# Zeros through the matrix engine, one group's statistics later, and batch norm rows widened by another engine

## The chip, the cores and the metric

The kernel runs on one core of a Trainium2 chip. A core has a matrix engine (TensorE, PE in the profile), a vector engine (VectorE, DVE), a scalar engine (ScalarE, ACT), a general engine (GpSimd, POOL) and a queue engine (SyncE, SP) that here only issues DMAs; ACT and POOL issue DMAs too. PE reads its operands from the on-chip memory SBUF and writes its products to [...]another one, PSUM, from which DVE and ACT take them away. The metric is device time in microseconds of one execution of the whole program.

## The reference

The input is `x`, 128 samples of 128 nodes with 256 channels, in float32, and an adjacency matrix for each sample. Two layers follow one another, each of the form `x = x + f(relu(layernorm(x)))`. Cut to its first part, which is all that the change touches, the first layer is

```python
h  = relu(layernorm(x))                     # per node, over 256 channels
c  = relu(bn1(conv1d(h, conv1_w, width 1))) # a 256x256 product per node
c  = bn2(conv1d(c, conv2_w, width 17))      # a convolution along the nodes
xc = relu(c + h)                            # then messages, a GRU, the second layer
```

`bn1` multiplies each output channel by a scale and adds a shift. Everything after (messages along an adjacency computed from the data, a GRU, and a second layer of five small graph convolutions) is unchanged.

## The kernel before, in words

The samples go in groups of four, numbered q = 0 to 31; sixteen groups make a batch (`bat`). The width-17 convolution is done in the frequency domain: stage A brings a batch into it, stage B multiplies there, and a third stage goes back and does everything else.

**Stage A, for one group** (`stage_a`, L390 to L443). SP loads the group's input into a tile `xa` (four DMAs of 128 KB, L382; four such tiles exist, so group q+4 takes the place of group q). `moments` (L265 to L275) computes mean and variance on DVE, four pairs of instructions, and the inverse root on POOL (L274); `normalize` (L277) applies them on DVE. PE transposes the group (`ph`, L411), ACT applies the ReLU into `hTa` (L413, two tiles, each of which POOL also stores to DRAM, L416), PE multiplies by the width-1 weights `c1w` (`pc`, L422), DVE adds the shift row `brow` (L425), ACT applies the ReLU (L427), PE multiplies by the Fourier matrix (`pf`, L433), and DVE and ACT copy the result into `X` (L439, L441).

**Before the first group** `fold` (L282 to L307) works bn1 into `c1w`. The scale and the shift stand as columns (one number per partition) and are needed as rows. So DVE widens each of four columns to 128x128 (`wide`, L301), PE multiplies it with the identity (`prow`, L302), DVE multiplies `c1w` by the scale rows (L306) and copies the shift rows to `brow` (L307). `fold` also computes the moments of group 0 and normalises it (L303).

**Beside stage A** `tap_weights` (L461) brings the 17 taps of the second convolution into the frequency domain: 32 steps of four products (`pw`, L477), in four rounds of eight. The taps of round n are loaded into one of two tiles `wt` by SP and POOL (`load_taps`, L452), so those of round 2 can be loaded only when the last products of round 0 are done. POOL stores the results (`wfd`, L489).

**The order** of all this is planned on the host. Each program (`stage_a(q)` of up to three groups, `tap_weights`) is a Python generator that issues instructions and then yields two numbers, the PE time that it has just used and the time after which it wants to be asked again. A planner (`Order`, L176) keeps a clock of its own from these numbers and asks whichever program is due. [...]The line that concerns us is in `stage_a`: a group that has no moments yet computes them when it is asked (L397 to L402), and the load of group q+1 is issued when group q starts (L392).

Of the kernel before, what the change touches and what calls it, by code (L numbers as in the profile page):

```python
# [9 lines left out]
FP = mybir.dt.float32  # L10
AF = mybir.ActivationFunctionType
# [4 lines left out]
B, N, D = 128, 128, 256  # L16
# [3 lines left out]
P = 128  # L20
# [187 lines left out]
def kernel(ctx: ExitStack, tc: tile.TileContext, x, adj, consts, vecs, w_se, conv1_w,  # L208
                    conv2_w, w_msg, b_msg, w_ih, w_hh, W1, W2, b2, fusion_w, out):
    nc = tc.nc  # L210
# [7 lines left out]
    ptmp = ctx.enter_context(tc.tile_pool(name="ptmp", bufs=5, space=PSUM))  # L218
# [15 lines left out]
    def c(name):  # L234
        a, b = CAT[name]
        return cst[:, a:b]

    def v(name, i=None):
        a, b = VAT[name]
        return vec[:, a:b] if i is None else vec[:, a + i:a + i + 1]  # L240
# [24 lines left out]
    def moments(src, tag):  # L265

        st = f2.tile([P, 4, 6], FP, tag=tag + "st", name="st", bufs=4)
        mv = f2.tile([P, 4, 2], FP, tag=tag + "mv", name="mv", bufs=4)
        rs = f2.tile([P, 4], FP, tag=tag + "rs", name="rs", bufs=4)
        for t in range(4):  # L270
            nc.vector.bn_stats(st[:, t], src[:, t])
            nc.vector.bn_aggr(mv[:, t], st[:, t])
        nc.vector.tensor_scalar(rs, mv[:, :, 1], EPS, None, op0=ALU.add)
        nc.gpsimd.tensor_tensor(rs, rs, c("mhalf")[:, :4], ALU.pow)  # L274
        return mv, rs  # L275

    def normalize(dst, src, mv, rs):  # L277
        for t in range(4):
            nc.vector.tensor_scalar(dst[:, t], src[:, t], mv[:, t, 0:1], rs[:, t:t + 1],
                                    op0=ALU.subtract, op1=ALU.mult)  # L280

    def fold():  # L282


        s = cp.tile([P, 4], FP, name="s_bn")
        t = cp.tile([P, 4], FP, name="t_bn")
        for i, bn in enumerate(("bn1", "bn2")):
            scl[bn], sft[bn] = s[:, 2 * i:2 * i + 2], t[:, 2 * i:2 * i + 2]
            nc.vector.tensor_scalar(scl[bn], v(bn + "_v"), EPS, None, op0=ALU.add)
        nc.gpsimd.tensor_tensor(s, s, c("mhalf")[:, :4], ALU.pow)  # L290
        MOM[0] = moments(XA[0], "a")
        load_taps(0, nc.gpsimd, nc.sync)
        for bn in ("bn1", "bn2"):
            nc.vector.tensor_mul(scl[bn], scl[bn], v(bn + "_g"))
            nc.vector.tensor_mul(sft[bn], v(bn + "_m"), scl[bn])
            nc.vector.tensor_sub(sft[bn], v(bn + "_b"), sft[bn])
        prow = ptmp.tile([P, 4, P], FP, tag="tmp", name="prow")
        wide = tw.tile([P, 4, P], FP, tag="wide", name="wide", bufs=1)
        for i, a in enumerate((scl["bn1"][:, 0:1], scl["bn1"][:, 1:2], sft["bn1"][:, 0:1],
                               sft["bn1"][:, 1:2])):  # L300
            nc.vector.tensor_copy(wide[:, i], a.to_broadcast([P, P]))  # L301
            nc.tensor.matmul(prow[:, i], wide[:, i], ident, start=True, stop=True)  # L302
        normalize(XA[0], XA[0], *MOM[0])  # L303
        nc.vector.tensor_add(brz, v("b_ih")[:, 0:4], v("b_hh")[:, 0:4])
        for k in range(2):
            nc.vector.tensor_mul(c1w[:, k], c1w[:, k], prow[:, 0:2].rearrange("p a c -> p (a c)"))  # L306
        nc.vector.tensor_copy(brow, prow[:, 2:4].rearrange("p a c -> p (a c)"))  # L307

    def fold_gates():

# [58 lines left out]
    brow = xf.tile([P, D], FP, name="brow")  # L369
# [15 lines left out]
    def load_xa(q):  # L385
        if q not in XA:
            XA[q] = LATE["ab"].tile([P, 4, D], FP, tag="xa", name=f"xa{q}", bufs=4)
            load_x(XA[q], q)

    def stage_a(q):  # L390
        ab = LATE["ab"]
        for n in range(q, min(q + 2, (q // BQ + 1) * BQ)):  # L392
            if n not in XA:
                load_xa(n)
                if n == q:
                    yield 0.0, 14.0 if q > BQ else 6.0
        if q not in MOM:  # L397
            if BQ < q < BQ + 3:
                yield 0.0, 11.0 * (q - BQ) - 10.0
            MOM[q] = moments(XA[q], "a")  # L400
            yield 0.0, 3.0
            normalize(XA[q], XA[q], *MOM[q])  # L402
            yield 0.0, 2.0
        while q - 2 >= q // BQ * BQ and q - 2 not in A_DONE:
            yield 0.0, 0.5
        xn = XA[q]
        hT = ab.tile([P, 2, 512], FP, tag="hTa", name=f"hTa{q}")
        for cc in range(2):
            ph = ptmp.tile([P, 4, GB, WIDE], FP, tag="tmp", name=f"ph{q}_{cc}")
            for t in range(4):  # L410
                nc.tensor.transpose(ph[:, t].rearrange("p j n -> p (j n)"),  # L411
                                    xn[:, t, cc * P:(cc + 1) * P], ident)
            nc.scalar.activation(  # L413
                hT[:, cc].rearrange("p (j t n) -> p t j n", j=GB, t=4), ph, AF.Relu)
        yield 0.9, 2.4
        nc.gpsimd.dma_start(out=hTd[q], in_=hT)  # L416
        h1 = ab.tile([P, GB, D], FP, tag="h1", name=f"h1{q}")
        for h in range(2):
            pc = ptmp.tile([P, 2, D], FP, tag="tmp", name=f"pc{q}_{h}")
            for i in range(2):  # L420
                for k in range(2):
                    nc.tensor.matmul(pc[:, i], hT[:, k, (2 * h + i) * N:(2 * h + i + 1) * N],  # L422
                                     c1w[:, k], start=(k == 0), stop=(k == 1))
            s = slice(2 * h, 2 * h + 2)
            nc.vector.tensor_tensor(h1[:, s], pc, brow[:, None, :].to_broadcast([P, 2, D]),  # L425
                                    ALU.add)
            nc.scalar.activation(h1[:, s], h1[:, s], AF.Relu)  # L427
            yield 1.75, 2.8 * h
        for h in range(2):
            for k in range(2):  # L430
                pf = ptmp.tile([P, 2, D], FP, tag="tmp", name=f"pf{q}_{k}_{h}")
                for i in range(2):
                    nc.tensor.matmul(pf[:, i, :F * NB], h1[:, 2 * h + i, k * P:(k + 1) * P],  # L433
                                     fwd, start=True, stop=True)
                g0 = (q % BQ * GB + 2 * h) * NB
                dst = X[:, k, :, g0:g0 + 2 * NB].rearrange("p f (g b) -> p f g b", b=NB)
                src = pf[:, :, :F * NB].rearrange("p g (f b) -> p f g b", b=NB)
                if (k, h) == (0, 0):
                    nc.vector.tensor_copy(dst, src)  # L439
                else:  # L440
                    nc.scalar.activation(dst, src, AF.Copy)  # L441
            yield 1.1, 0.0
        A_DONE.add(q)  # L443
# [3 lines left out]
    tws = [mid.enter_context(tc.tile_pool(name=f"tws{i}", bufs=1)) for i in range(3)]  # L447
    tw = mid.enter_context(tc.tile_pool(name="tw", bufs=2))
    wse = tw.tile([P, 2, 67], FP, tag="wse", name="wse", bufs=1)
    wts = []  # L450

    def load_taps(n, *engines):  # L452

        wt = tw.tile([P, 16, D], FP, tag="wt", name=f"wt{n}")
        src = conv2_w.rearrange("(r n i) t o -> n t r i o", r=4, n=4)[n]
        for r in range(4):
            engines[r % len(engines)].dma_start(out=wt[32 * r:32 * r + 16], in_=src[:16, r])
        engines[0].dma_start(out=wt[16::32], in_=src[16])
        wts.append(wt)
# [727 lines left out]
    load_xa(1)  # L1187
    load_xa(2)
    fold()
    beside = Lane([tap_weights()] + [early(q) for q in range(NQ)])  # L1190
    gates = Lane([fold_gates(), fold_fusion()], weight=0.5)
    for bat, (during_a, during_b) in enumerate(((0.66, 0.5), (0.2, 0.65))):
        if bat:
            take_turn("ab", 2, reuse_waits="tile")
        begin = Lane([stage_a(q) for q in range(bat * BQ, (bat + 1) * BQ)], ahead=3)
        beside.weight = during_a
        order.run(begin, beside, *[gates] * bat, until=begin)
        take_turn("xw", 3, reuse_waits="tile")
        products = Lane([stage_b(bat)])
        beside.weight = during_b  # L1200
        order.run(products, beside, *[gates] * bat, until=products)
# [52 lines left out]
```

## Time and profile before

| | |
|---|---|
| time, median of 3 runs | 2012.26 us (2009.02 to 2017.96) |
| time of the profiled execution | 2009.44 us |
| its span, first to last instruction | 2007.7 us |
| PE busy | 1960.1 us, 98% of the span |
| DVE, ACT, POOL busy | 67%, 34%, 33% |
| first product of the kernel's own (`prow`) | 9.93 us from the span's start |
| first product of stage B (`pa`) | 190.35 us |

Times inside the profile are counted in microseconds from the start of the span. A row of the order of time gives the start, the time until the last of the merged instructions ends, engine, line, operation, output and input; a bracket gives how long the engine had been idle and what released it. SPq and POOL rows named DMA_DIRECT2D are the issuing of a DMA, not its transfer. One float32 product appears as two PE records.

### The profile page before, as it was taken

To read this page: it belongs to the slowest core of one execution; us is meant where nothing else is said; L and a number is where in the kernel's file an instruction comes from. 1 tells how busy PE (TensorE), PEld (TensorE's weight loads), DVE (VectorE), ACT (ScalarE), POOL (GpSimd) and SP (SyncE) were. 2 spreads that over 40 slices of the span, in tenths; PEclk is the share of its full clock that TensorE was granted. 3 is DMA by queue.
4 is the path that set the end of the run, shared out by engine and by line. 5 is a ranking of instruction groups with operands and counts; after the bars stand their busy time and mean duration, and the time that the engine had idled before them with its cause. 6 is when DMAs were issued, how large, how long until landed. Compare 5 with 4: busy or idle time off the path is not lost.

```text
span 2007.7 us, 33356 instructions
## 1 busy us (share of the span) xinstructions
PE 1960.1 (98%) x12598; PEld 1625.4 (81%) x12598; DVE 1352.3 (67%) x3002; ACT 683.4 (34%) x1547; POOL 655.7 (33%) x897
## 2 busy tenths in 40 slices
PE   7999999999999999999999999999999999999998
PEld 5667888889888888878778878888888888888865
DVE  6775445885433576885885787778668867886652
ACT  4664222454222344222323232232323332322233
POOL 3452666332656111241331232222221322222320
PEclk9999999999999999999999999999999999999999
DMA  9997879744887743542433342443442433433331
GB/s 212 296 273 250 274 250 289 220 148 158 269 258 254 198 124 107 163 103 82 119 90 108 106 113 77 118 112 88 118 121 80 126 102 98 107 102 108 65 94 53
DMA packets 184106, 302.88 MB, mean 151 GB/s; under 512 B 28501, under 2 KB 131994, under 8 KB 183690
## 3 DMA queue, kind: packets, MB, share of 16 engines
q1 hardware_dynamic: 138762, 168.81, 28.9%
q0 software_dynamic: 44800, 131.66, 22.6%
q8 instruction: 100, 1.64, 0.3%
q14 instruction: 60, 0.49, 0.1%
q10 hardware_dynamic: 384, 0.28, 0.1%
HBM read 204.12 MB, written 109.05 MB: 156 GB/s over the span
## 4 chain that ended last, share of the span: by engine, by line
PE 87%; DVE 7%; DMA 3%; issue 1%; ACT 1%; SPq 1%; POOL 0%; DVEq 0%; ACTq 0%; POOLq 0%
PE p L755 41%; PE pa L531 7%; PE ph L1110 5%; PE pz L1119 5%; PE pm L642 5%; PE pc L422 4%; PE pb L531 3%; PE px L668 3%; PE pf L433 3%; PE pi L712 3%; PE pw L477 1%; PE py L1093 1%; PE ph L411 1%; DMA xa<-in_x 1%; PE pse L626 1%
## 5 line engine op out<-in xcount | busy, mean ns | idle before, releaser
L938 POOL DMA_DIRECT2D x1d<-xt x128 | 101.1, 815 | 467.2 <-DVE xt L936 454.9
L837 POOL DMA_DIRECT2D xt<-in_x x128 | 100.2, 789 | 173.8 <-DMA x1d<-xt 166.8
L563 DVE SCALAR_TENSOR_TENSOR y<-pa,kk 128x512 f32<-128x512 f32 x78 | 53.8, 690 | 151.2 <-ACT kk L562 151.1
L531 PE MATMUL pa<-wf,X 128*128 128x256 f32 x640 | 152.2, 381 | 0.0
L755 PE MATMUL p<-th,wrz 128*128 128x256 f32 x512 | 134.5, 385 | 0.0
L755 PE MATMUL p<-tc,wrz 128*128 128x256 f32 x512 | 131.4, 379 | 0.0
L755 PE MATMUL p<-tm,wrz 128*128 128x256 f32 x512 | 131.4, 379 | 0.0
L531 PEld LDWEIGHTS pa<-wf,X 128*128 128x128 f32 x640 | 118.1, 190 | 16.2 <-issue 2.0
L422 PE MATMUL pc<-c1w,hTa 128*128 128x256 f32 x512 | 121.2, 383 | 2.7 <-DVE X L439 1.5
L642 PE MATMUL pm<-wmsg,hT 128*128 128x256 f32 x512 | 121.5, 382 | 0.0
L1110 PE MATMUL ph<-yz,w 128*128 128x96 f32 (+3 forms) x640 | 109.3, 325 | 1.4 <-DVE yz L1095 1.4
L422 PEld LDWEIGHTS pc<-c1w,hTa 128*128 128x128 f32 x512 | 94.0, 191 | 19.9 <-DVE h L425 4.8
L755 PEld LDWEIGHTS p<-th,wrz 128*128 128x128 f32 x512 | 94.7, 190 | 19.1 <-issue 7.3
L1112 ACT ACTIVATE hh<-ph,vec 128x96 f32<-128x96 f32 (+3 forms) x160 | 63.6, 401 | 133.5 <-PE ph L1110 125.1
L724 ACT ACTIVATE xc<-xc,t_bn 128x256 f32<-128x256 f32 x128 | 58.2, 500 | 148.5 <-DVE xc L721 148.5
L755 PEld LDWEIGHTS p<-tc,wrz 128*128 128x128 f32 x512 | 97.3, 190 | 13.9 <-issue 0.8
L642 PEld LDWEIGHTS pm<-wmsg,hT 128*128 128x128 f32 x512 | 95.8, 190 | 15.2 <-ACT kk L562 1.4
L1119 PE MATMUL pz<-hh,w 128*128 128x96 f32 (+3 forms) x640 | 107.5, 322 | 0.7 <-DVE yz L1121 0.7
L755 PEld LDWEIGHTS p<-tm,wrz 128*128 128x128 f32 x512 | 97.3, 190 | 13.2
L1110 PEld LDWEIGHTS ph<-yz,w 128*128 128x128 f32 x640 | 88.3, 193 | 22.4 <-issue 15.6
L1119 PEld LDWEIGHTS pz<-hh,w 128*128 128x128 f32 x640 | 86.3, 191 | 18.6 <-DVE yz L1121 1.3
L755 PE MATMUL p<-hTc,wrz 128*128 128x256 f32 x384 | 99.3, 381 | 1.2 <-DVE z L829 1.2
(204 smaller groups left out, 4464.8 us busy)
## 6 DMA issues: line engine op xcount, KB each, us to landing
wf<-wfd SPq DMA_DIRECT2D x160, 256.0 KB
wfd<-ws POOLq DMA_DIRECT2D x64, 320.0 KB, 10.2
yd<-y POOLq DMA_DIRECT2D x80, 256.0 KB, 4.0
yt<-yd SPq DMA_DIRECT2D x64, 320.0 KB
w<-in_W SPq DMA_DIRECT2D x40, 512.0 KB
xa<-in_x SPq DMA_DIRECT2D x128, 128.0 KB
hTd<-hTa POOLq DMA_DIRECT2D x32, 512.0 KB, 6.6
hT<-hTd SPq DMA_DIRECT2D x32, 512.0 KB
```

Of the source, the lines that this page charges most:

```text
L422: nc.tensor.matmul(pc[:, i], hT[:, k, (2 * h + i) * N:(2 * h + i + 1) * N], c1w[:, k], start=(k == 0), stop=(k == 1))
L433: nc.tensor.matmul(pf[:, i, :F * NB], h1[:, 2 * h + i, k * P:(k + 1) * P], fwd, start=True, stop=True)
L531: nc.tensor.matmul(ps, xk(k), WF[f][:, k, s], start=(k == 0), stop=(k == 1))
L642: nc.tensor.matmul(pm[:, i], hT[:, k, j * N:(j + 1) * N], LATE["wmsg"][:, k], start=(k == 0), stop=(k == 1))
L668: nc.tensor.matmul(px[:, dc, i], msgs[h][:, i, dc * P:(dc + 1) * P], aT[:, 2 * h + i], start=True, stop=True)
L712: nc.tensor.matmul(pi[w * WIDE:(w + 1) * WIDE, :, :, n].rearrange("p k g c -> p g k c"), inv[:F, o:o + WIDE], yt[:, n // 2::2].rearrange(" ...
L755: nc.tensor.matmul(ps[:, m], w[:, i, k, m * P:(m + 1) * P], factor(i, x, t), start=first and j == 0, stop=last and j == len(n) - 1, skip_g ...
L837: nc.gpsimd.dma_start(out=xt[a * WIDE:(a + 1) * WIDE].rearrange("p b d c -> p (b d) c"), in_=slices(x[q * GB:(q + 1) * GB])[a])
L938: nc.gpsimd.dma_start(out=slices(x1d[q])[a], in_=xt[a * WIDE:(a + 1) * WIDE].rearrange("p b d c -> p (b d) c"))
L1110: nc.tensor.matmul(ph, w1[:, k, m * P:(m + 1) * P], yz[:, k, :, o:o + n], start=(k == 0), stop=(k == 1))
L1112: nc.scalar.activation(hh[:, m], ph, AF.Relu, bias=v("b1", g * 4 + m))
L1119: nc.tensor.matmul(pz, w2[:, g, m, cc * P:(cc + 1) * P], hs[g][:, m], start=(m == 0), stop=(m == 3))
```

## The change

Three edits, all in what runs before and during stage A of the first batch.

```diff
 def fold():
-            nc.vector.tensor_copy(wide[:, i], a.to_broadcast([P, P]))
+            nc.scalar.activation(wide[:, i], a.to_broadcast([P, P]), AF.Copy)
             nc.tensor.matmul(prow[:, i], wide[:, i], ident, start=True, stop=True)
...
-        nc.vector.tensor_copy(brow, prow[:, 2:4].rearrange("p a c -> p (a c)"))
+        nc.scalar.activation(brow, prow[:, 2:4].rearrange("p a c -> p (a c)"), AF.Copy)
...
 def stage_a(q):
         if q not in MOM:
+            if q == 2:
+                yield 0.0, 7.0
             if BQ < q < BQ + 3:
                 yield 0.0, 11.0 * (q - BQ) - 10.0
             MOM[q] = moments(XA[q], "a")
...
     wse = tw.tile([P, 2, 67], FP, tag="wse", name="wse", bufs=1)
     wts = []
+    idle = tws[2].tile([P, 4, 4, D], FP, tag="ws", name="idle")[:, 0, :3]
+    nc.gpsimd.memset(idle, 0.0)
+    pidle = ptmp.tile([P, 2, D], FP, tag="tmp", name="pidle")
+    for _ in range(5):
+        nc.tensor.matmul(pidle, idle[:, 2, :P], idle[:, :2], start=True, stop=True)
```

The four widenings and the copy to `brow` go from DVE to ACT. The group of index 2 waits seven units of the planner's clock before its moments are issued. And five products of zeros, 128x512 each, are issued to PE ahead of everything else; their result is read by nobody.

Because the planner decides with a running clock, the second edit also changes the order of what follows. In the program that is built, PE's order differs from the kernel before in its first 140 or so of 2868 rows (through the first rows of the third round of taps, all within stage A of the first batch) and is the same after that. In SP's queue, the load of group 7 now stands behind the loads of the taps of round 2, where it stood ahead of them; group 9 stands ahead of the late constants (L253 to L255) and group 11 ahead of the taps of round 3, where they stood behind them. In DVE's queue, the moments of group 7 stand directly after those of group 6 and ahead of the two additions of `brow` (L425) of group 5; the moments of group 10 stand directly after those of group 9.

## The prediction

> **What bounds the kernel now.** The page first: PE is busy in 98% of the span, and its chain of what ended last is 87% PE.
>
> ```profile
> span 2007.7 us, 33356 instructions
> PE   7999999999999999999999999999999999999998
> DMA  9997879744887743542433342443442433433331
> ```
>
> One slice is 50 us. So a microsecond of PE idleness saved or added early moves the end by as much; only the first slice has room; and there the DMA engines are as full as PE. Second, the order of time of the first 25 us.
>
> ```profile
> 9.66 0.36 DVE L301 COPY wide<-s_bn 128x128 f32<-128x128 f32 x2
> ...
> 9.93 2.08 PE L302 MATMUL prow<-cst,wide 128*128 128x128 f32 x8 [9.93 <-DVE wide L301]
> ...
> 12.05 0.75 DVE L306 TENSOR_TENSOR c1w<-c1w,prow 128x256 f32<-128x256 f32 x2 [0.32 <-PE prow L302]
> 12.72 0.42 DVE L307 COPY brow<-prow 128x256 f32<-128x256 f32 x1
> 13.05 0.42 DVE L271 BATCH_NORM_STATS2 st<-xa 128x6 f32<-128x256 f32 x1
> ...
> 15.48 0.43 DVE L271 BATCH_NORM_STATS2 st<-xa 128x6 f32<-128x256 f32 x1
> ...
> 17.82 0.68 DVE L425 TENSOR_TENSOR h<-pc,brow 128x512 f32<-128x512 f32 x1
> 18.42 2.66 DVE L279 TENSOR_SCALAR xa<-xa,mv,rs 128x256 f32<-128x256 f32 x8
> ...
> 21.00 0.68 DVE L425 TENSOR_TENSOR h<-pc,brow 128x512 f32<-128x512 f32 x1
> ...
> 27.59 1.04 PE L411 MATMUL ph<-cst,xa 128*128 128x128 f32 x8
> ```
>
> From 12 to 21.7 DVE sets the pace: two groups' moments (2.43 us each, 13.05 to 15.48 to 17.91) and eight normalisations stand before the additions that PE's group 1 needs; its `pc` starts at 22.89. From there PE is dense. Third, the queue engine, its order of time and its waits between 40 and 60 us.
>
> ```profile
> 28.65 13.45 SPq L382 DMA_DIRECT2D xa<-in_x  x8
> 57.69 1.26 SPq L457 DMA_DIRECT2D wt<-in_conv_w  x2
> 58.99 0.74 SPq L458 DMA_DIRECT2D wt<-in_conv_w  x1
> 59.83 2.13 SPq L382 DMA_DIRECT2D xa<-in_x  x4
> ...
> SPq L457 <- PE pw L477: 15.4, 1, 15.4
> ```
>
> SP stands 15.4 us before the taps of round 2, until PE's last product of round 0 (57.5). In this kernel groups 6 and 7 were loaded ahead of that wait; group 8 is the one behind it. Fourth, DVE after the taps of round 3, where the same happens to group 11:
>
> ```profile
> 112.36 0.43 DVE L271 BATCH_NORM_STATS2 st<-xa 128x6 f32<-128x256 f32 x1 [1.91 <-DMA xa<-in_x]
> ```
>
> PE lost 1.7 us to that at 113.5 and 0.8 at 117.
>
> **What the Trainium skill says.** "TensorE: Matmul & The Clock Gate", Part 1: PE's clock is halved until a window of about 3.4 us has been busy, and again after an idle one. The trace agrees: eight records of 128 columns took 2.08 us at 9.93 and 1.04 at 27.59; the granted-clock records begin full speed at 14.7 and show half speed for 3.4 us at 171.7, after 3.60 us of waiting. The same page (architectural detail) calls DVE and ACT strict FIFO. "Trainium Kernel Development and Optimization", Key Constraints: DMAs of SP, ACT and POOL share 16 engines and interleave. The trace: while POOL's stores ran (78 to 84 us) SP's queue moved 82 to 96 KB/us, alone (60 to 66) 130. "ScalarE: Activation LUTs", What ACT_TABLE_LOAD costs: 186 ns + 0.833 per element, 293 ns for 128; the trace's nearest row (aT, 128x128) has 281.
>
> **The change part by part.** Against the profiled execution (2009.44 for a span of 2007.7).
>
> *Zeros.* A memset of 768 columns on POOL, by the row of 848 columns (858 ns) 0.8 us, is done by about 1.5; POOL's next work is at 5.16. Five products of 512 columns: eight `pc` records of 256 take 1.82 us start to start, so a product of 512 takes 0.91, cold 1.8; together 4.6 to 9.1, over at 7 to 10.6, and `prow` is due at 9.3. If they wake the clock, `prow` and the first `ph` run at full speed; but `prow` is then awaited by nobody (DVE normalises group 0 until 11.4) and `ph` waits for that normalisation. Worth 0.3 us, between +0.7 (zeros late, clock cold) and -0.8. The PSUM bank and the `ws` tile that they use are next wanted long after.
>
> *ACT for DVE.* DVE loses four copies (0.54) and `brow` (0.42). ACT is idle there until 12.90; four at 0.28 start when the scale is ready (8.9) and end near 9.85. DVE normalises group 0 at 9.95 to 11.4 (POOL's root ends 9.92), scales `c1w` at 11.5 to 12.2 and begins group 1's moments at 12.2, not 13.05.
>
> *Statistics later.* Group 1's moments end at 14.6; `pc` of group 0 is ready (14.3), first addition to 15.3, normalising group 1 (root until 15.7) to 17.1, second addition to 17.75 where it was 21.68. ACT: ReLU 18.4, two `hTa`; `pc` of group 1 at 19.0 instead of 22.89, **3.9 us**. Group 2's moments then fill 17.8 to 20.2, its normalisation 21.6 to 23.0, before `ph` at 23.7. The first `pw` is due at 24.65, and its taps (a POOL DMA issued at 11.2, 13.6 us to landing) come near 25.0: 3.5 left. In the new order `ph` of group 4 no longer waits for its normalisation (1.59 instead of 0.95 at 46.85) and a few tenths more are found: the last `pw` of round 0 ends near 53.1 instead of 57.5, **-4.4**.
>
> *The planner's other moves.* Call that end T. SP now waits until T for the taps of round 2, and **group 7 is behind them**, not ahead. The packet records of before show that 576 packets of taps and 512 of group 8 took from T+1.3 to T+10.7 with POOL's queue empty for most of it, because its next stores waited until T+4.4. After, POOL issues them from T+1 (no moments between), and their packets flow some 4 us later: SP's queue has the engines alone to about T+5, then 80 to 90 KB/us. I get the last packet at T+11.3 and the landing at **T+12** (10.5 if the engines stay free, 20 at the pace of round 3, where taps and group 11 took 19.5 us of packets). DVE reaches group 7's moments at T+8.1 and waits. Behind them stand both additions of group 5, and behind those ACT and PE's `pf` of group 5, which PE reaches at T+9.0 (two pairs of `pf` 2.38, `ph` 0.93, two steps of `pw` 2.06, two `pc` 3.64). It gets its data at landing + 2.4 + 0.7 + 0.7 + gaps, T+16.1: **+7.1** of idleness, and half speed for 3.4 us after it, **+1.7**. Then: `hTa` of group 7 needs the store of group 5, whose issue by POOL is behind group 7's root (+1, between 0 and 3); `ph` of group 9 waits for two groups' moments back to back (+2.1). Gone are the waits of before at 79.9 (0.9) and 86.6 (0.7) and, since group 11 is now loaded ahead of round 3's taps, those of group 11 (2.5).
>
> Sum: -4.4 + 7.1 + 1.7 + 1.0 + 2.1 - 0.9 - 0.7 - 2.5 = +3.4. Nothing later is reordered, and PE carries the shift to the end. The profiled execution is 2.8 under the median, so I add to the median: **2015 us**, the same within 0.5% (10 us), which is about what can be told from no change.
>
> **The rivals.**
>
> *A: the late load is covered.* If group 7 lands by T+7, or DVE's order has slack that I don't see, only gains stay: -4.4 - 0.9 - 0.7 - 2.5 + 2.1 = -6.4, 2006. For it: POOL's earlier stores are over at about T+1. Against: SP's wait for T is in the trace, and 1.1 MB must come after it; at 130 KB/us that alone is 8.4 us.
>
> *B: the load of group 7 is starved (the other side).* POOL's stores and taps, 1.8 MB, take the engines as in round 3: landing at T+20, idleness 15, sum +11.3, 2024, slower by over 0.5%. It decides from a landing at T+19. For it: the DMA row is at 9 here. Against: POOL's stores can't all be ready that early.
>
> *C: the zeros don't do what they say*, zeros not counting as activity or another phase of the window: at most 0.7 us more; cannot be told from the forecast by time.
>
> **How the numbers follow.** Forecast 0.62 (landing T+10 to T+15: 2011 to 2019 with 2 us of run noise to each side), A 0.22, B 0.14, C 0.02. A reaches over 0.5% faster only if the 3.6 us wait for the adjacency at 168 shrinks too: 0.05 faster. Of B about two thirds lie above 2022: 0.09 slower; the rest, 0.86, same. Range 2004 to 2023: it leaves out the tail of A and the upper half of B.
>
> **What would show it.** Right: `pc` of group 1 near 19 us; the last `pw` of round 0 near 53; a PE idleness of 5 to 10 us near 62 to 69 before `pf`, with DVE waiting for a DMA of `xa`; records at half speed after it; no wait of DVE for `xa` near 112; first `pa` at about 193. Early `prow` records at 0.13 instead of 0.26 us show the zeros. Wrong: DVE not waiting at group 7, or `pc` of group 1 later than 20.5.

## The result and the profile after

| | before | after |
|---|---|---|
| median of 16 runs each, on the same chip | 2013.45 us (2009.02 to 2021.11) | 2022.82 us (2017.91 to 2029.63) |
| profiled execution | 2009.44 us | 2018.64 us |
| its span | 2007.7 us | 2016.9 us |
| first product of stage B (`pa`) | 190.35 us | 198.37 us |

The ratio after to before is 1.0043, with a 95% interval of 1.0029 to 1.0057. The changed kernel is slower by 0.43%, some 9 us. That is inside the half per cent that the forecast counted as the same, though the interval reaches beyond it. The median of 2022.82 is 0.2 us inside the upper end of the forecast's range (2004 to 2023), and outside the 2011 to 2019 of its main case. The forecast was +2.8 us on the median of three runs (its own sum, +3.4, gives 2015.7, not 2015); the medians of sixteen differ by 9.4 and the profiled executions by 9.2. So the sign of the sum was right, and its size was a third of what was measured.

First the page of the changed kernel.

```profile
span 2016.9 us, 33374 instructions
PE   9799999999999999999999999999999999999998
DMA  9898878744777744543433343343443433343331
```

The first slice of PE has gone from 7 to 9 (the zeros fill it, and work has come forward), the second from 9 to 7. What the second slice lost is in the order of time. TensorE's start:

```profile
1.52 6.83 PE L457 MATMUL pidle<-idle 128*128 128x512 f32 x10 [1.52 <-POOL idle L454]
9.60 1.16 PE L302 MATMUL prow<-cst,wide 128*128 128x128 f32 x8 [1.25 <-ACT wide L301]
...
19.39 2.05 PE L424 MATMUL pc<-c1w,hTa 128*128 128x256 f32 x8
...
25.43 1.18 PE L484 MATMUL pw<-wt,cst 17*80 17x512 f32 x8 [0.30 <-DMA wt<-in_conv_w]
...
28.50 0.70 PE L424 MATMUL pc<-c1w,hTa 128*128 128x256 f32 x2 [0.61 <-ACT hTa L415]
```

The zeros run from 1.52, full speed begins at 6.13 us by the granted-clock records (14.66 before), and `prow` takes 1.16 us where it took 2.08. The `pc` of group 1 starts at 19.39; it was 22.89. Below it stand two waits. The first, 0.30 us for the first taps, the forecast had (it expected them near 25.0). The second, 0.61 us for `hTa` of group 2, it had not. ACT's order of time tells what that one is:

```profile
27.85 1.09 ACT L415 ACTIVATE hTa<-ph 128x512 f32<-128x512 f32 x2 [2.20 <-DMA hTd<-hTa]
```

There are two `hTa` tiles, so group 2 writes into the one that POOL has stored for group 0, and ACT stood 2.20 us for that store. Now the place of the loss. SP's order of time:

```profile
54.81 2.06 SPq L464 DMA_DIRECT2D wt<-in_conv_w  x2
56.92 1.46 SPq L465 DMA_DIRECT2D wt<-in_conv_w  x1
58.47 13.98 SPq L382 DMA_DIRECT2D xa<-in_x  x12
```

SP issues the taps of round 2 as soon as the last `pw` of round 0 ends (at 54.6, the forecast's time T), and group 7 behind them. POOL issues the last stores of round 0 and its own half of those taps at the same time:

```profile
55.57 2.02 POOL L496 DMA_DIRECT2D wfd<-ws  x4 [1.44 <-ACT ws L489]
57.70 1.17 POOL L464 DMA_DIRECT2D wt<-in_conv_w  x2
```

VectorE's order of time has the landing:

```profile
72.32 0.43 DVE L271 BATCH_NORM_STATS2 st<-xa 128x6 f32<-128x256 f32 x1 [9.65 <-DMA xa<-in_x]
```

and TensorE's what it costs:

```profile
62.53 1.10 PE L484 MATMUL pw<-wt,cst 17*80 17x512 f32 x8
76.07 2.50 PE L435 MATMUL pf<-cst,h 128*128 128x160 f32 x8 [12.44 <-ACT h L429]
78.50 2.01 PE L484 MATMUL pw<-wt,cst 17*80 17x512 f32 x8
80.44 1.97 PE L413 MATMUL ph<-cst,xa 128*128 128x128 f32 x8
82.20 2.34 PE L435 MATMUL pf<-cst,h 128*128 128x160 f32 x8
84.47 1.16 PE L484 MATMUL pw<-wt,cst 17*80 17x512 f32 x8
```

VectorE waits 9.65 us for group 7's input. The two additions of group 5 have their products since PE's `pc` ahead of 62.53, but they stand behind the moments that wait; this agrees with the strict order that the forecast cited for VectorE. So PE's `pf` of group 5 comes after 12.44 us of nothing. Then `pw`, `ph` and `pf` take 2.01, 1.97 and 2.34 us where the same rows take 1.10, 1.09 and 1.25 elsewhere. The table of stretches of the same kernel gives the clock; its columns are the stretch and its length, the busy time of PE, PEld, DVE, ACT and POOL with instruction counts, then granted clock, share of the DMA engines and GB/s.

```profile
60.00:76.07 16.07, 3.63 (x22) 2.17 (x20) 6.08 (x22) 0.73 (x3) 2.21 (x3) 0.74 0.91 249
76.07:84.64 8.57, 8.57 (x36) 6.33 (x40) 6.94 (x21) 5.19 (x11) 3.86 (x6) 0.50 0.74 232
84.64:110.00 25.36, 24.47 (x147) 16.57 (x148) 15.89 (x39) 14.99 (x31) 8.83 (x15) 1.00 0.87 222
```

From 60 us to the end of the wait the DMA engines are 91% busy. Whose transfers these are, the packets of each queue tell. From 55 to 59 us POOL's queue, with stores issued before T at first, had 90% of the engines' time and moved 0.91 MB; SP's, with the taps, had 6% and moved 0.08 MB. From 60 to 67 us POOL's moved 1.64 MB and SP's 0.51 MB, in nearly as many packets (485 and 545), since POOL's had 3.4 KB each and SP's 0.9. Only after that had SP's queue the engines nearly to itself. And for 8.57 us after the wait PE works at exactly half speed, which costs half of that, 4.3 us.

Two more places count in the sum. At group 9 PE waits for `ws`, and half speed follows from 111.94 to 115.36:

```profile
109.27 2.12 PE L484 MATMUL pw<-wt,cst 17*80 17x512 f32 x8 [0.89 <-DVE ws L491]
```

And ahead of stage B the kernel before waits for the adjacency (first row), the changed kernel doesn't (second row):

```profile
171.83 1.12 PE L657 MATMUL pd<-cst,adj 128*128 128x128 f32 x4 [3.60 <-DMA adj<-in_adj]
180.79 0.66 PE L664 MATMUL pd<-cst,adj 128*128 128x128 f32 x4
```

### The profile page after: what moved, and what is told of

It is laid out like the page before. It is cut to its first block, busy times and chain, and to the rows that moved or that the text cites. A ratio compares the mean times of both kernels' runs of the same rounds, so it can differ in the third digit from the quotient of the medians.

```text
span 2016.9 us, 33374 instructions
## 1 busy us (share of the span) xinstructions
PE 1969.1 (98%) x12608; PEld 1630.5 (81%) x12608; DVE 1351.0 (67%) x2997; ACT 686.8 (34%) x1552; POOL 655.2 (32%) x898
## 3 DMA queue, kind: packets, MB, share of 16 engines
q8 instruction: 100, 1.64, 0.4%
## 4 chain that ended last, share of the span: by engine, by line
PE 90%; DVE 6%; DMA 2%; ACT 1%; issue 1%; SPq 0%; POOL 0%; DVEq 0%; ACTq 0%
PE p L762 41%; PE pa L538 7%; PE ph L1117 5%; PE pz L1126 5%; PE pm L649 5%; PE pc L424 4%; PE pb L538 3%; PE pf L435 3%; PE px L675 3%; PE pi L719 3%; PE pw L484 2%; PE ph L413 1%; PE py L1100 1%; DMA xa<-in_x 1%; PE pse L633 1%; PE pg L1160 1%
## 6 DMA issues: line engine op xcount, KB each, us to landing
xa<-in_x SPq DMA_DIRECT2D x128, 128.0 KB
```

## The experiments

The theory: the late statistics of group 2 move group 7's load behind the taps of round 2, where POOL's stores and its own half of the taps compete with it; the rest of the change gains about what was worked out. The rivals: the zeros or the copies on ACT cost something themselves; POOL's traffic has nothing to do with the landing; the slowness behind the wait isn't the clock. A good place to compare kernels is the first product behind stage A (`pbs`, L338, beside the last group's `ph`), since orders differ only ahead of it. Times of `pbs` and `pa` are those of one profiled execution per kernel. In the six kernels whose order on PE is the same up to there (changed, group 7 ahead, POOL's traffic held back, both with dense products, moments later) the last `pw` of round 0 starts between 52.94 and 53.87 us, so a difference of under 1 us between two of these times says little. Medians and ratios are of all runs, each beside the kernel before on the same chip, which had 2013.2 to 2013.8 us there; chips differ from group to group.

| kernel | `pbs` at | first `pa` at | median, us | ratio to before, 95% interval |
|---|---|---|---|---|
| before | 156.73 | 190.35 | 2013.45 | |
| changed | 169.36 | 198.37 | 2022.82 | 1.0043 (1.0029 to 1.0057) |
| zeros and ACT, no delay | 156.23 | 187.82 | 2013.44 | 0.9996 (0.9978 to 1.0014) |
| delay alone | 169.84 | 198.84 | 2019.86 | 1.0032 (1.0019 to 1.0044) |
| group 7 ahead of the taps | 159.41 | 188.43 | 2010.47 | 0.9997 (0.9979 to 1.0014) |
| POOL's traffic held back | 163.43 | 192.44 | 2019.00 | 1.0020 (1.0009 to 1.0032) |
| twelve dense products | 170.13 | 204.94 | 2020.23 | 1.0040 (1.0026 to 1.0053) |
| seventeen dense products | 165.75 | 194.76 | 2018.94 | 1.0030 (1.0016 to 1.0045) |
| late statistics, old order | 158.35 | 188.53 | 2010.94 | 0.9996 (0.9975 to 1.0017) |
| the same, group 11 earlier | 150.74 | 184.87 | 2011.31 | 0.9984 (0.9965 to 1.0002) |
| group 7 ahead, moments later | 157.28 | 193.8 | 2010.18 | 0.9983 (0.9969 to 0.9997) |

**Which part.** The changed kernel without the delay, and the kernel before with the delay alone:

```diff
# without the delay, against the changed kernel; with it alone, the same lines added to the kernel before
         if q not in MOM:
-            if q == 2:
-                yield 0.0, 7.0
```

> The change without the seven planner units before group 2's moments: zeros and the copies on ScalarE alone, so every queue keeps the order of the kernel before. If the loss comes from group 7's load behind the wait of SP (theory), nothing is lost here: no idleness of PE between 60 and 80 us beyond the 0.9 us that the kernel before has at 79.9, and a time between 2 us below and 1 us above the kernel before, because DVE saves about 1 us at the start. If the zeros or the copies on ScalarE themselves cost something later (rival), the time is 3 to 9 us above the kernel before.

> The kernel before with the seven planner units alone. Theory: the whole loss is here, 8 to 11 us above the kernel before (the changed kernel's 9 and up to 1 more for the lost microsecond at the start), with PE idle for 11 to 14 us near 64 to 77 and DVE waiting for group 7's load. Rival (the other two edits matter): within 4 us of the kernel before.

The first has its `pc` of group 1 at 21.68, 1.2 us ahead of the kernel before, and no wait at group 7. The second shows VectorE's wait by itself:

```profile
72.89 0.43 DVE L271 BATCH_NORM_STATS2 st<-xa 128x6 f32<-128x256 f32 x1 [9.27 <-DMA xa<-in_x]
```

PE stood 12.06 us behind it, and the half clock of 17.07 us is there too. Its `pbs` is within 0.5 us of the changed kernel's. So at `pbs` the whole of the loss is the two lines of the delay. By all runs the delay alone costs 6.1 us, less than the 8 to 11 expected, and its interval overlaps that of the changed kernel. Zeros and ACT gain at `pbs` only 0.5 us in either pairing (156.73 to 156.23, 169.84 to 169.36), which is too little to be told from nothing: the 1.2 us at group 1 shrink before they arrive.

**Order or traffic.** One kernel issues group 7's load ahead of the taps of round 2, as it stood before. The other leaves the order of SP and takes POOL's traffic away: four stores and POOL's half of those taps go into POOL's queue behind group 7's root.

```diff
# group 7 ahead
+                    if n == 1:
+                        load_xa(7)
                     load_taps(n + 1, nc.sync, nc.gpsimd)
# POOL's traffic held back: the four stores at (n, m) == (0, 7) and the odd parts of
# the taps of round 2 are put into a list, and issued at step (1, 1)
+                if (n, m) == (1, 1):
+                    for out, part in HELD:
+                        nc.gpsimd.dma_start(out=out, in_=part)
```

> The changed kernel with one thing moved: SP issues group 7's load ahead of the taps of round 2; the order on every other engine is the same. Theory: the 12.4 us of idleness and the 4.3 us lost at half clock after it go, other waits stay about as they are (hTa of group 7 may wait up to 3 us for its store), so 13 to 17 us below the changed kernel: about 2006 to 2010, below the kernel before too. Rival (DVE's order, two groups' moments back to back, is what stops PE): at most 4 us below the changed kernel.

> The changed kernel with POOL's four stores of the last tile of round 0 and POOL's half of the taps of round 2 held back behind group 7's root, so that SP's queue has the DMA engines nearly alone while taps and group 7 come in; nothing else moves. If POOL's traffic is what made the landing T+17.7 instead of the T+12 of the forecast, group 7 lands between T+10 and T+13, PE idles 5 to 8 us instead of 12.4, and the time is 4 to 8 us below the changed kernel. If the landing is late for another reason (rival), it stays above T+16 and the time within 2 us of the changed kernel.

With POOL's traffic held back, VectorE gets group 7 at 67.48, after 5.44 us of waiting, and PE stands 8.23 us instead of 12.44, both just outside what was expected (the landing is T+13.5, T being 54.0 here; the time is 3.8 us below the changed kernel's):

```profile
67.48 0.43 DVE L271 BATCH_NORM_STATS2 st<-xa 128x6 f32<-128x256 f32 x1 [5.44 <-DMA xa<-in_x]
```

Some of what is gained is not the traffic's: SP began its taps 0.64 us earlier in this profile (54.17). From there to the landing it is 13.3 us, against 17.5 in the changed kernel. So the traffic held back, stores and taps together, made 4.2 us of the lateness; which of the two made more was not tried. Nor are the other 13.3 SP's alone. POOL's earlier stores, issued by 53.5 and not held back, were still moving: from 54.3 to 58 us POOL's queue had 90% of the engines' time and SP's 10% (0.09 MB), and SP's moved 1.6 MB from there to the landing.

With group 7 ahead of the taps VectorE does not wait for a load at all, and yet PE stands:

```profile
62.35 1.10 PE L486 MATMUL pw<-wt,cst 17*80 17x512 f32 x8
66.25 1.35 PE L435 MATMUL pf<-cst,h 128*128 128x160 f32 x8 [2.80 <-ACT h L429]
67.53 2.76 PE L486 MATMUL pw<-wt,cst 17*80 17x512 f32 x8
```

The same kernel's VectorE has the reason. Group 7's moments run from 62.50 to 64.84, straight after those of group 6, and the additions of group 5 start then:

```profile
62.50 0.43 DVE L271 BATCH_NORM_STATS2 st<-xa 128x6 f32<-128x256 f32 x1
...
64.84 1.29 DVE L427 TENSOR_TENSOR h<-pc,brow 128x512 f32<-128x512 f32 x2
```

So 2.80 us of the 12.44 come from VectorE's order alone, whenever the load lands; the late load makes the other 9.6. Even the short wait left a half clock for 6.83 us. By all runs this kernel is at 2010.47 us, just above the 2006 to 2010 expected, and cannot be told from the kernel before.

**Is it the clock?** Dense products that nobody uses fill the wait ahead of `pf`; if PE is slow afterwards because it stood still, the slowness must go. Twelve were too few, seventeen fill it (the expectations call `pf` the two-row products):

```diff
     # stage_a, ahead of the pf products
+        if q == 5:
+            pwarm = ptmp.tile([P, 2, D], FP, tag="tmp", name="pwarm")
+            for _ in range(17):     # the first of the two kernels: range(12)
+                nc.tensor.matmul(pwarm, c1w[:, 0, :P], c1w, start=True, stop=True)
```

> The changed kernel with twelve products of 512 columns (real operands, result read by nobody) put into PE's queue where it idles before pf of group 5. They take 10.2 to 11 us of the 12.4 us of waiting, so the wait itself is not lengthened. If the slowness after the wait (76 to 84.6 us, every product at twice its time) is the halved clock after idleness, the records show no half-speed stretch near 68 to 85 and the time is 3 to 5 us below the changed kernel, about 2018. If the products there are slow for another reason, or if the idleness ends later than the clock matters, the time is within 1 us of the changed kernel.

> The changed kernel with seventeen dense products of 512 columns put into PE's queue right ahead of group 5's two-row products, so that they fill the whole of the wait for h (12.44 us in the changed kernel; the twelve of the earlier experiment took 10.57 us and left 2.94 us open behind them). They compute nothing that is used. Theory: the slowness behind the wait is the halved clock, and it is halved because PE stood still. Then no half-speed stretch stands between 65 and 90 us; the products take about 15 us, 2 to 3 more than the wait, so that the two-row products begin at about 78.5 instead of 76.07, and the work behind them takes about half as long as it did (8.6 us became 4.3). In sum stage B begins 1 to 3 us earlier than in the changed kernel, at 195.5 to 197.5 us. Rival: the work behind the wait is slow for another reason (reads of freshly written data, shared PSUM), then it stays as slow, and stage B begins 2 to 3 us later, at about 201.

The twelve ended 2.94 us before `h` came, and a half clock of 6.83 us followed from 78.37: so it does not decide. Its first `pa` at 204.94 is no measure of the edit either, since that profile, of the longest execution of its kernel, lost another 3.52 us to the adjacency at 185.1, with a half clock of 6.83 us. The seventeen leave no gap:

```profile
63.43 14.86 PE L434 MATMUL pwarm<-c1w 128*128 128x512 f32 x34
78.13 1.25 PE L439 MATMUL pf<-cst,h 128*128 128x160 f32 x8
79.31 1.10 PE L488 MATMUL pw<-wt,cst 17*80 17x512 f32 x8
...
82.45 1.10 PE L488 MATMUL pw<-wt,cst 17*80 17x512 f32 x8
```

The `pf` products begin 2.06 us later than in the changed kernel (78.13 against 76.07), and the last `pw` shown, the same one that stood at 84.47, begins 2.02 us earlier. That is 4.1 us for the clock, against 4.3 from the table of stretches. The window of half speed near 112 is gone as well, though the wait of 0.89 us ahead of it is still there; the first `pa` comes 3.6 us earlier, more than the 1 to 3 expected. The slowness is the halved clock.

**The late statistics without the planner's other moves.** The delay is taken out, and group 2's moments and normalisation are put by hand behind the additions of groups 0 and 1, so that nothing later moves. The second kernel also loads group 11 ahead of the taps of round 3, as the changed kernel does.

```diff
-        if q not in MOM:
-            if q == 2:
-                yield 0.0, 7.0
+        if q == 2 or q not in MOM:      # same yields, but group 2 issues nothing here
...
+            if (q, h) == (0, 1):
+                MOM[2] = moments(XA[2], "a")
+            if (q, h) == (1, 0):
+                normalize(XA[2], XA[2], *MOM[2])
# the second kernel, in addition
+                    if n == 2:
+                        load_xa(11)
                     load_taps(n + 1, nc.sync, nc.gpsimd)
```

> All three edits, but group 2's moments and normalisation are put by hand where the changed kernel has them (after the second addition of group 0, after the first of group 1) and the planner sees its old numbers, so PE, SP and everything after the first 25 us keep the order of the kernel before. Theory: the gain of the start, 3 to 4 us at pc of group 1, is kept, nothing is lost at group 7, and the time is 2 to 5 us below the kernel before. Rival (stage A is held by DMA, so a microsecond found at the start is given back at the next load or store): the start is earlier by the same 3 to 4 us, but stage B begins within 1.5 us of the kernel before and the time is the same.

> The same with group 11's load put ahead of SP's wait for the taps of round 3, the one good that the planner's new order had done. Theory: the wait of DVE for group 11 (1.9 us near 112, 2.5 us of PE with what follows) goes as well, so stage B begins another 1.5 to 3 us earlier and the time is 4 to 8 us below the kernel before. Rival (held by DMA): the wait only moves to group 12 or to the adjacency at 168, and stage B begins no earlier than without it.

The first keeps group 1's gain and has no wait at group 7, but loses 3.60 us at 114.36, where group 11 comes late, and works at half clock for 6.83 us after it: at `pbs` it is 1.6 us behind the kernel before, so there its rival came out (the gain is given back at a later load), and by all runs the time is the same. The second has nothing of either, and is at `pbs` at 150.74, 6.0 us ahead of the kernel before; there the rival did not come out. It waits for the adjacency, as the kernel before does,

```profile
165.18 1.11 PE L670 MATMUL pd<-cst,adj 128*128 128x128 f32 x4 [2.94 <-DMA adj<-in_adj]
```

with a half clock of 6.83 us around it, and `pa` comes 5.5 us ahead. Over all runs the ratio is 0.9984, and its interval ends at 1.0002: the gain of some 3 us is less than the 4 to 8 expected and cannot be told from nothing.

**What is left of the wait with group 7 ahead.** Group 7's moments go behind the additions of group 5.

```diff
# group 7 ahead, and in stage_a
-            MOM[q] = moments(XA[q], "a")
+            if q != 7:
+                MOM[q] = moments(XA[q], "a")
...
+            if (q, h) == (5, 1):
+                MOM[7] = moments(XA[7], "a")
```

> The kernel with group 7's load ahead of the round's weights, and in addition group 7's moments behind the two additions of group 5 in VectorE's order, not ahead of them. Theory: what was left of the wait at 66 us (2.80 us, and the half clock of 6.83 us behind it that costs 3.4) came from VectorE taking two groups' moments back to back ahead of the additions that the two-row products wait for. Then that wait and that half-speed stretch are gone, and stage B begins 4 to 6 us earlier than with the load alone moved, at 182.5 to 184.5 us; the whole takes 2004 to 2007 us, a ratio of 0.996 to 0.998 to the kernel before. Rival: group 7's moments are then late for its own transposes, the wait returns there, and stage B begins within 1.5 us of 188.4.

The cause of that wait is confirmed: 0.36 us are left of it, and no half clock follows.

```profile
63.96 1.35 PE L438 MATMUL pf<-cst,h 128*128 128x160 f32 x8 [0.36 <-ACT h L430]
...
169.66 6.23 PE L654 MATMUL pm<-wmsg,hT 128*128 128x256 f32 x16 [4.57 <-DMA wmsg<-in_w_msg]
```

The size is not: of 5.8 us (2.44 of wait and 3.4 of half clock) only 2.1 are left at `pbs`. The lead over the kernel with group 7 ahead was 4.5 us at 70.6; a wait of 1.17 us for `ws` at 80.28 and a half clock from 82.64 took it down to 0.7; 1.5 came back where that kernel has a half clock at 102.29 and this one has none. Then this execution stood 4.57 us for the message weights, and its first `pa` came at 193.8, 9 us after the latest time expected. It was the longest of its kernel, at 2022.29 us against a median of 2010.18, which is itself 3 us above the range expected. By the runs, this is the only kernel whose interval lies below 1: 0.9983, 0.9969 to 0.9997. That is narrow for the best of ten kernels, so its 3 us on the kernel before are likely rather than shown; against the changed kernel it is some 12 us by the two ratios.

## Why the prediction was right, and where it was wrong

- **What the change moves: right.** Group 7 behind the taps, VectorE waiting for `xa`, the additions of group 5 behind it, `pf` idle, half speed after, no wait for group 11: all stand where they were put. The delay alone gives the loss, and the load put back takes most of it away (9.95 of the 12.6 us at `pbs`).
- **The start, -4.4: measured -2.9** (last `pw` of round 0 ends at 54.6, not 57.5). Group 1's `pc` gained 3.5 of the 3.9, and at the first `pw`, where 3.5 were forecast, 3.1 were left (25.43 against 28.55). Then 1.0 was lost to a buffer, so that the second `pw` is 2.1 ahead (30.48 against 32.59): the step counted what VectorE and PE release, not that `hTa` of group 2 needs POOL's store of group 0 to be done. That store was issued 3.1 us earlier than before (15.86) and took 11.9 us where it had taken 9.4, so it landed only 0.6 us earlier. The wait ahead of group 4's `ph` did go, which makes 2.9. Rival C is out by the profile, not by the time: the clock was full at 6.13 us and `prow` halved.
- **The idleness, +7.1: measured +12.4.** This is the step that failed. When VectorE and PE reach the wait was right (VectorE at T+8.1, PE at T+9.0). The landing was put at T+12; it came at T+17.7, close to rival B's T+19. The step that was wrong is "SP's queue has the engines alone to about T+5": up to T+4.4 it had 6% of them. The stores that POOL had issued before T were put down as over at about T+1, but they kept the engines until about 59 us, nearly as late as in the kernel before (59.5), though T came 2.9 us earlier. That is the part that is still there with POOL's later traffic held back: T+13.5, where 10.5 had been put down for free engines, so 3.0 of the 5.7 us by which the landing was missed. (That it was these stores is read from the packets; no run moved them.) The other 2.7 are the later traffic, which was priced at 1.5 us (12 against 10.5) and made 4.2. "POOL's stores can't all be ready that early" was wrong too: the four stores were issued from 55.57, the taps by 58.9. The Trainium skill states the sharing in "Trainium Kernel Development and Optimization", Key Constraints, without a size; these numbers agree, and the forecast's size was too small.
- **The half clock, +1.7: measured +4.3**, shown by the seventeen products. The step took one window of 3.4 us. PE worked 8.57 us at half speed; after the 8.23 us of waiting with POOL's traffic held back it was 9.5. "TensorE: Matmul & The Clock Gate", Part 1, speaks of at least one busy window of about 3.4 us until full speed. The start took one whole window and what was left of the one before (4.6 us from the first zeros). The return after the wait took two whole windows and a rest, so here the measurement decides.
- **Two groups' moments back to back (group 9), +2.1: measured +3.8.** The size of the wait was right, but it is `pw` that waits, for `ws`, which VectorE copies behind the moments, and not `ph`: 0.89 us lie ahead of the row at 109.27, the rest inside it (2.12 us where 1.10 is usual). The half clock at 111.94 adds 1.7, which the forecast hadn't. **`hTa` of group 7, +1.0: 0**, no such wait is in the profile. **The waits gone, -4.1:** as counted, and a fourth one of the kernel before, which the forecast didn't count, went too: 0.7 us at 128.0, where `ph` took 1.69 us.
- **"PE carries the shift to the end": wrong, to the kernel's favour.** The terms above give -2.9 + 12.4 + 4.3 + 3.8 - 4.1 - 0.7 = +12.8, and `pbs` was 12.6 later. But the kernel before waited 3.60 us for the adjacency, and the changed one, which gets there later, did not. With the half clock that the kernel before has there (up to 1.7 us) this gives back 4.6 us net, and `pa` comes only 8.0 later. The last 1.2 of the 9.2 us lie beyond stage B, where kernels with two or three windows of half speed differ by as much (1817.1 to 1818.5 us from the first `pa` to the end); their cause stays open. A forecast with every early term right would have said about +12.6 and been 3 us too high, so the time stayed inside the range by luck: the wait at the adjacency, which the forecast left out, gave back half of what the early terms lacked. Nor is that load in time by itself: with twelve dense products `pbs` stood at 170.13, and PE still waited 3.52 us for the adjacency.
- **Rival A** ("DVE's order has slack that I don't see") is refuted for both its reasons: the load landed at T+17.7 and not by T+7, and with the load early 2.80 us of wait and a half clock stay, because the double moments alone hold the additions back. **Rival B** was nearer than the forecast by time (2024 against 2022.82), though its landing at T+20 didn't come.

## What to carry to other kernels

Where a planner decides the order, a delay of one small step is a change to every queue: list what it moves in each DMA queue, and price a load that falls behind a wait by all that other queues have under way and will issue in that same moment, not by the rate when they are silent. Work that comes forward doesn't bring the transfers before it forward: here PE's wait for round 0 ended 2.9 us earlier, and POOL's stores held the engines until 59 us all the same. On an engine with a strict order, put a statistic that waits for a load behind the work that is ready. And count a gain only up to the next wait for a load whose time is set elsewhere: here the adjacency and the message weights took 1.6 to 4.6 us from each of the five kernels that left stage A before 158.4 us, and 3.5 us from one of the six that left it later.

## What the runs showed of the hardware that was not expected

- **The clock returns slowly.** After idleness of 12.44 and 8.23 us TensorE worked for 8.6 and 9.5 us (`pf`, transposes, products over 17 rows) before it had full speed again; after one of 2.80 us it went on at full speed for 1.9 us and was then halved for 6.83. Dense zeros at the start needed 4.6.
- **The clock changes on a grid.** In each of the eleven profiles all granted-clock records begin on a grid of 3.413 us (its start differs from profile to profile), and within the program half speed lasts 1, 2, 4 or 5 of its steps (3.41, 6.83, 13.65, 17.07 us). In the changed kernel it lasts from 67.57 to 84.64. PE came back at 76.07, within a step that began at 74.40, so the 8.57 us are the rest of that step and two whole ones; with POOL's traffic held back the 9.5 us come out the same way. How busy a step must be is not shown.
- **Single windows of half speed at places without a long wait.** Beyond stage B the profiles show between 2 and 7 such windows of 3.41 us (not counting the last microseconds of the span), most at like places (near 375, 785, 875, 935, 1270, 1505, 1660, 1925), each worth some 1.7 us by its length. From the first `pa` to the end of the span it is 1817.3 us with two of them (before), 1818.5 with three (changed), 1822.5 with five (group 7 ahead) and 1826.7 with seven (group 7 ahead, moments later). This code is the same in all kernels. What sets their number stays open: it is why a gain of 5.5 us at stage B in one profile could be 2 us of loss at its end, and why stage times were compared here and not spans.
